# Projections of a fused LayerNorm, attention and LoRA layer: GpSimd in program order, T sums one product ahead, fixed places for the own sums, token operands stored one transfer at a time

## The chip, the cores and the metric

The kernel runs on one core of a Trainium2 chip. The metric is the device time of one launch in microseconds; the median of three runs counts. All arithmetic is in float32.

The engines are named as in the profile: PE multiplies matrices (PEld loads its stationary operand), DVE, ACT and POOL (GpSimd) work on elements, and SP issues most of the transfers (DMAs). Each engine takes its instructions in a fixed order and waits on semaphores.

## The reference

```python
xn = layernorm(x)                       # x: 4 x 512 x 1024
qkv = xn @ w_qkv                        # 32 query heads, 8 key/value heads of 128
scores = einsum(q, k) * 128**-0.5 - slope * sqrt(distance)   # causal
attn = softmax(scores) @ v @ w_o        # grouped heads
ffn = xn @ W.T + b + LoRA(xn)           # rank 8, 16, 32 or 64 by the top gate
out = x + attn + ffn
```

## The kernel before, in words

The kernel has three parts one after the other: `project()` (LayerNorm, the gate and the projections to q, k and v), `attend()` (attention) and `finish()` (W and w_o). The change lies in the first part, and in two loads of the second.

**Two levels of Strassen-Winograd.** Each large product is computed from seven products of half size instead of eight, and each of those again. The outer level works on a pair of batches (1024 tokens): the products are numbered 1 to 7 and taken in the order `PROJECTED`, (1, 2, 6, 3, 7, 4, 5). The inner level makes seven multiplications out of each product: class `Inner`, methods m1 to m7, each of them four 128x128 by 128x256 matrix instructions in the profile. `run()` (L172) calls them in the order m1, m5, m4 of the product before, m6, m3, m2, m7, and calls `beside()` after each. So a product is seven multiplications, and a *set* is seven products, 49 multiplications. There are 24 sets, twelve for each pair of batches: for each two key/value heads one set "kv" (keys in column 0, values in column 1), then two sets "q".

**Sums.** Winograd's scheme needs sums of operands:
- *outer sums of tokens*: `Pair.outer` and `Pair.inner`, on DVE (one on POOL), once for a pair; a1 to a7 and their inner sums stay in SBUF for the twelve sets.
- *outer sums of weights*: `outer_w` (L494), eight DVE operations of 128x512 in a set, in tiles `to` and in place in `w`.
- *T sums*: `inner_w` (L513), four POOL operations of 128x256 for each product, in the tile `ti`, which has three buffers. In the version before, `item()` (L526) calls it when the product begins.
- *read-outs*: an inner product's results are read from PSUM by ACT (`scalar.copy`) where there is no base (products 1 and 5), else added to the base by DVE (L127). Product 5 is also added to u and v by POOL, quarter by quarter (L564).

PSUM has two banks for each of the kinds c, d and a. m6 and m7 and m4 accumulate into the bank that m1, m6 and m7 have left, so they wait until that was read out.

**Work put beside the products.** `beside()` (L603) takes steps from queues of generators, so the place of everything in the program is fixed by counting multiplications:
- `soon`: token sums and the transposes of the first pair, on two of three multiplications.
- `weights`: outer sums of weights, a step on each third multiplication.
- `later`: a step on each sixth (`pace[1]`). In it are the routing of each batch, `put_by` (L439) for each of the seven outer operands of a pair (it stores the operand and its inner sums to DRAM, tiles `s`, for `finish()`), and the eight tiles of the second pair (`tile_of_second`, L667: load, LayerNorm, transposes, low rank, store). When product 1 of set 11 is finished, `flush(later)` (L844) emits all that is left of it at once.
- `apart`: two generators `weights_put_by` (L685), turn 0 with its sums on POOL and turn 1 on DVE. They make the *own sums*: sums of W and w_o that `finish()` will want. There are 55 pieces for each. A piece is a load to a tile `wr`, a pause of five multiplications, four sums of 128x256, and a store to `t` or `m`. POOL's are held back during products 1 and 5 (`pace[4]`), DVE's on each third multiplication. They run in sets 1 to 10 and 13 to 23 (`pace[3]`).
- `delayed`: `in_while(n, f)` calls f n multiplications later: loads of the next set's weights `w` (2 MB), stores of q, k and v.

**Order of the engines.** `project()` keeps PE and SP in program order from the start; DVE is added after set 1 (`in_order`, L771, entered at L848). POOL's order is chosen at compile time by the scheduler of the language, from its own estimates; only the own sums and their transfers, under `pin`, keep their order among themselves.

## Time and profile before

| what | us |
|---|---|
| median of three runs | 2808.44 (2808.34 to 2816.88) |
| the profiled execution's own time | 2813.63 |
| its span | 2811.8 |
| PE busy over the span | 2631.7 (94%) |
| POOL busy | 1912.9 (68%) |
| DVE busy | 1766.8 (63%) |
| end of the projections, start of attention | about 1220 |
| mean granted clock of PE | 0.977 |

In what follows a *row* of a timeline has: start in us, duration in us, engine, line, operation, output and input by the program's names, shapes, count, and in brackets the idle time of the engine ahead of it and what ended it. A row of transfers has: output and input, the queue, count, size of one, and the median time in us from issue to landing. Tile names: `ti` T sums, `to` outer sums of weights, `wr` own sums, `s` stored token operands, `xi` and `x` token operands, pc, pd and pa the PSUM banks.

### The profile page before, as it was taken

The page shows a single profiled execution, that of the slowest core. Times are in us where ns is not written, and L with a number is a line of the kernel's source. Part 1 is how long each engine was busy: PE and PEld are TensorE (multiplying, and loading weights), DVE is VectorE, ACT ScalarE, POOL GpSimd, SP SyncE. Part 2 cuts the span into 40 slices and gives each one's busy share as a digit, 9 for nine tenths or more (in the row PEclk, how much of TensorE's full clock was granted, in tenths as well). Part 3 has the DMA queues.
Part 4 walks back from the last instruction along what each step waited for, and adds up shares of the span by engine and source line. Part 5 has one row for each costly group of instructions (what it writes and reads, how often), then busy time and mean ns, then how long its engine had stood idle before and what let it go on. Part 6 is the DMA issues. An engine that isn't in the chain of part 4 may idle for free.

```text
span 2811.8 us, 35613 instructions
## 1 busy us (share of the span) xinstructions
PE 2631.7 (94%) x11872; PEld 2091.1 (74%) x11872; DVE 1766.8 (63%) x3636; ACT 651.4 (23%) x1727; POOL 1912.9 (68%) x1973
## 2 busy tenths in 40 slices
PE   7779999988899999989999999999599999999998
PEld 6668888877778888856666666666488888888887
DVE  6746666558566765546666666766565666566554
ACT  3001111110000000056666666664000000000000
POOL 3557877766687888647777777685566567666573
PEclk9989999989999999999999999999799999999999
DMA  3297777766776774235666666766978878788883
GB/s 131 99 349 243 249 248 239 242 199 217 257 251 229 242 238 157 90 124 174 198 216 198 213 213 199 232 236 198 324 267 311 286 276 324 227 310 295 303 293 122
DMA packets 385065, 648.06 MB, mean 230 GB/s; under 512 B 22569, under 2 KB 285481, under 8 KB 375666
## 3 DMA queue, kind: packets, MB, share of 16 engines
q1 hardware_dynamic: 382130, 638.70, 66.6%
q10 hardware_dynamic: 2752, 7.08, 0.7%
q8 instruction: 95, 1.56, 0.2%
q14 instruction: 88, 0.72, 0.1%
HBM read 387.74 MB, written 257.96 MB: 230 GB/s over the span
## 4 chain that ended last, share of the span: by engine, by line
PE 50%; POOL 5%; DMA 5%; DVE 3%; issue 2%; SPq 1%; ACT 0%; POOLq 0%; ACTq 0%; DVEq 0%
PE pc L1161 11%; PE psc L925 9%; PE po L963 9%; PE pd L1161 5%; PE ptr L950 3%; PE pa L1161 3%; PE pc_q L534 3%; DMA sa<-s 2%; DMA w<-in_w_o_dram 1%; POOL t L130 1%; PE pc_kv L534 1%; PE pd_q L534 1%; DVE pt L953 1%; DVE p L930 1%; PE pd_kv L534 1%
## 5 line engine op out<-in xcount | busy, mean ns | idle before, releaser
L939 POOL TENSOR_SCALAR p<-p,tot 128x256 f32<-128x256 f32 (+3 forms) x512 | 315.5, 635 | 150.6 <-DVE tot L937 93.1
L925 PE MATMUL psc<-k,q 128*128 128x512 f32 (+3 forms) x1024 | 307.5, 439 | 8.2 <-DMA q<-q 7.1
L930 DVE CUSTOM_DVE_ANT_0 p<-psc,bias 128x256 f32<-128x256 f32 (+3 forms) x512 | 245.3, 491 | 104.1 <-PE psc L925 80.3
L130 POOL TENSOR_TENSOR t<-w 128x640 f32<-128x640 f32 x96 | 191.5, 1995 | 171.5 <-DMA w<-in_w_o_dram 74.8
L934 ACT ACTIVATE p<-p,low 128x256 f32<-128x256 f32 (+3 forms) x512 | 283.8, 555 | 72.1 <-DVE low L930 62.5
L963 PE MATMUL po<-pt,v 128*128 128x512 f32 x640 | 290.6, 592 | 0.0
L925 PEld LDWEIGHTS psc<-k,q 128*128 128x128 f32 x1024 | 173.6, 191 | 108.5 <-issue 64.1
L130 POOL TENSOR_TENSOR t<-w,t 128x640 f32<-128x640 f32 x96 | 203.9, 2124 | 35.8 <-PE pc L1161 32.0
L130 POOL TENSOR_TENSOR wr<-wr 128x256 f32<-128x256 f32 x220 | 174.5, 793 | 69.3 <-DMA wr<-in_w_o_dram 24.2
L534 PE MATMUL pc_q<-x,ti_q 128*128 128x256 f32 x704 | 185.0, 386 | 28.8 <-DVE q L127 14.3
L950 PEld LDWEIGHTS ptr<-ident,p 128*128 128x128 f32 x1280 | 147.3, 141 | 73.2 <-issue 40.0
L963 PEld LDWEIGHTS po<-pt,v 128*128 128x128 f32 x640 | 116.8, 190 | 108.5 <-issue 99.2
L534 PE MATMUL pc_q<-xi,ti_q 128*128 128x256 f32 x640 | 169.1, 387 | 20.3 <-DVE q L127 11.3
L953 DVE COPY pt<-ptr 128x512 f32<-128x512 f32 x192 | 129.7, 683 | 83.6 <-PE ptr L950 83.4
L950 PE MATMUL ptr<-ident,p 128*128 128x128 f32 x1280 | 167.7, 274 | 6.0 <-DVE pt L953 4.6
L534 PEld LDWEIGHTS pc_q<-x,ti_q 128*128 128x128 f32 x704 | 134.5, 193 | 51.6 <-DVE q L127 15.5
L130 DVE TENSOR_TENSOR wr<-wr 128x256 f32<-128x256 f32 x220 | 126.5, 575 | 68.5 <-DMA wr<-t 23.3
L534 PEld LDWEIGHTS pc_q<-xi,ti_q 128*128 128x128 f32 x640 | 121.9, 193 | 43.0 <-POOL ti_q L130 13.4
L130 POOL TENSOR_TENSOR ti_q<-w_q 128x256 f32<-128x256 f32 x128 | 103.2, 823 | 69.1 <-PE pc_kv L534 34.0
L165 ACT COPY m<-pc 128x256 f32<-128x256 f32 x30 | 11.2, 372 | 595.1 <-PE pc L1161 595.1
L1161 PE MATMUL pc<-sa,w 128*128 128x256 f32 x480 | 113.8, 385 | 27.9 <-DMA sa<-s 27.9
L130 POOL TENSOR_TENSOR ti_q<-to_q 128x256 f32<-128x256 f32 x96 | 75.9, 803 | 77.9 <-PE pc_q L534 50.8
(296 smaller groups left out, 5857.4 us busy)
## 6 DMA issues: line engine op xcount, KB each, us to landing
sa<-s SPq DMA_DIRECT2D x96, 640.0 KB, 7.7
s<-ot SPq DMA_DIRECT2D x112, 384.0 KB, 5.0
m<-wr SPq DMA_DIRECT2D x70, 512.0 KB, 3.5
w<-m SPq DMA_DIRECT2D x28, 1280.0 KB, 6.9
w_q<-in_w_qkv_dram SPq DMA_DIRECT2D x16, 2048.0 KB, 10.8
q<-q SPq DMA_DIRECT2D x30, 1024.0 KB, 7.1
s<-os SPq DMA_DIRECT2D x48, 512.0 KB, 4.4
t<-wr SPq DMA_DIRECT2D x40, 512.0 KB, 4.1
```

The source lines that it names most:

```text
L130: return eng.tensor_tensor(dst, u, v, ALU.subtract)
L165: nc.scalar.copy(dst, src)
L534: nc.tensor.matmul(dst, ops_w[m][:, c, :], XI[i][m][:, c, :], start=start and c == 0, stop=c == 1, skip_group_check=True,)
L925: nc.tensor.matmul(sc[:, :n], Q[u][:, g, ts(i, P)], K[u][:, :n], start=True, stop=True)
L930: nc.vector.tensor_tensor_reduce(pr[:, g], sc[:, :n], bias[p, h][:, g, S - n :], -SCALE, BIG, ALU.add, ALU.min, low,)
L934: nc.scalar.activation(pr[:, g], pr[:, g], AF.Exp, bias=low, scale=-1.0, accum_out=tot[:, g : g + 1])
L939: nc.gpsimd.tensor_scalar(pr[:, g], pr[:, g], tot[:, g : g + 1], 1.0, ALU.mult, ALU.mult)
L950: nc.tensor.transpose(tr[:, ts(g, P)], PR[u, i][:, g, ts(j, P)], ident)
L953: nc.vector.tensor_copy(pt, tr)
L963: nc.tensor.matmul(po, V[u][:, j, :], PT[i, j], start=(j == 0), stop=(j == i))
L1161: nc.tensor.matmul(bk, w[:, k], x[:, k], start=start and k == 0, stop=stop and k == KB - 1, skip_group_check=True,)
```

## The change

It does these things, all in `project()` but the last:

1. POOL is added to the engines that keep program order.
2. T sums are written by `ahead()` one multiplication after the product *before* has begun (and for product 1 of a set, in product 5 of the set before); `item()` takes them from `inner`. Sets 0 and 1 begin without this.
3. `OWN` lists the multiplications of a set on which outer sums of weights are made; DVE's own sums are held back on just these. While `pace[0]` is 2 (the first two sets) an outer sum is made on each multiplication.
4. POOL's own sums are held back in product 1 and after the fourth multiplication of product 5, and the pause before a piece's store is three multiplications in place of one.
5. `put_by` gives each of its transfers a step of its own, and `later` takes a step on each fourth multiplication in place of each sixth. `routing` and `tile_of_second` get further empty steps; the store of `um` comes two steps after its tile is written.
6. k and v of two heads are stored by one transfer of [128, 2, 512] in place of two, and attention loads half of such a tile.

```diff
-    k_d = {(i, h): scratch(f"k{i}_{h}", [P, S]) for i in range(B) for h in range(NKV)}
-    v_d = {(i, h): scratch(f"v{i}_{h}", [P, S]) for i in range(B) for h in range(NKV)}
+    k_d = {(i, h): scratch(f"k{i}_{h}", [P, 2, S]) for i in range(B) for h in range(0, NKV, 2)}
+    v_d = {(i, h): scratch(f"v{i}_{h}", [P, 2, S]) for i in range(B) for h in range(0, NKV, 2)}
...
         nc.scalar.copy(umT[:RMAX], tr[:RMAX])
-        nc.sync.dma_start(out=um_d[bi], in_=umT)
...
                         nc.sync.dma_start(out=d[:, slot], in_=src)
+                        yield
                     nc.sync.dma_start(out=d[:, 4:7], in_=self.T[i][:, :3])
...
+            inner = {}
+
+            def ahead(st, i):
+                if i > 2:
+                    need_w(st, i)
+                inner[st, i] = inner_w(st, i)
...
-                ops_w = inner_w(st, i)
+                ops_w = inner.pop((st, i), None) or inner_w(st, i)
...
-                        for j in range(2):
-                            d = (k_d, v_d)[col][bi, h + j]
-                            nc.sync.dma_start(out=d, in_=t[:, j, :])
+                        nc.sync.dma_start(out=(k_d, v_d)[col][bi, h], in_=t)
...
-            pace = [1, 6, 0, False, False]
+            pace = [1, 4, 0, False, 0, 0]
+            OWN = (3, 5, 6, 7, 13, 17, 21, 25)
+
+            def own_sums():
+                return pace[2] - pace[5] in OWN
...
-                if pace[2] % 3 == 0:
+                if pace[0] > 1 or own_sums():
                     do(weights)
...
                 u = yield from route(bi)
                 yield
+                yield
                 umT = r4(f"umT_{bi}")[: RMAX + 1, 0, :]
                 masked(bank, bi, u, umT)
+                yield
+                yield
+                nc.sync.dma_start(out=um_d[bi], in_=umT)
                 yield
...
                 xn = xr
+                yield
                 yield
...
                     transposed(bank, xn, t, half, xt[:, half * HC : (half + 1) * HC, :])
                     yield
+                yield
                 low_rank(bank, t, lambda c: xt[:, c, :])
...
-                        while not pace[4] if turn == 0 else pace[2] % 3 == 0:
+                        while pace[2] > pace[4] if turn == 0 else own_sums():
                             yield
                         pin(sub(eng, w[:, k], w[:, u], w[:, v]))
                         yield
-                    yield
+                    yield from pause(3)
...
-            in_order = tc.manual_schedule(engines={PE, SP, DVE})
+            in_order = tc.manual_schedule(engines={PE, SP, DVE, POOL})
...
+                    pace[5] = pace[2]
                     for i in PROJECTED:
...
-                        pace[4] = i not in (1, 5)
+
+                        pace[4] = pace[2] + {1: 0, 5: 4}.get(i, 9)
+                        nxt = PROJECTED[PROJECTED.index(i) + 1 :][:1]
+                        if nxt:
+                            in_while(1, lambda st=st, j=nxt[0]: ahead(st, j))
+                        elif 0 < k < len(sets) - 1:
+                            in_while(1, lambda st=sets[k + 1]: ahead(st, 1))
                         yield item(st, i, accs[st])
...
-                queue.dma_start(out=K[u], in_=k_d[2 * p + bi, h])
+                queue.dma_start(out=K[u], in_=k_d[2 * p + bi, h - h % 2][:, h % 2])
                 queue.dma_start(out=Q[u], in_=q_d[2 * p + bi, h])
-                queue.dma_start(out=VT[u], in_=v_d[2 * p + bi, h])
+                queue.dma_start(out=VT[u], in_=v_d[2 * p + bi, h - h % 2][:, h % 2])
```

## The prediction

> **What bounds the kernel now.** I read the busy rows by stage first, then PE's waits in the projections, then the order of time around the longest of them, then what the SP queue waits for. The projections end at about 1220 us of a 2811.8 us span; the change touches nothing behind them but two loads of attention. In stages (columns: length, busy time of PE, PEld, DVE, ACT, POOL with counts, granted clock, DMA share, GB/s):
>
> ```profile
> 145.00:210.00 65.00, 45.96 (x191) 39.04 (x190) 27.63 (x60) 2.98 (x8) 32.59 (x45) 0.84 1.04 367
> 240.00:590.00 350.00, 336.69 (x1599) 291.25 (x1598) 231.70 (x511) 42.30 (x91) 279.08 (x355) 0.99 0.75 246
> 710.00:760.00 50.00, 40.66 (x176) 34.80 (x175) 25.67 (x55) 2.98 (x8) 32.35 (x41) 0.90 0.89 304
> ```
>
> See that PE bounds the stage (96% in the long middle), except in two short stretches where PE, DVE and POOL are all idle and only the DMA engines are full. There the row says transfers, not arithmetic. PE's waits, projections only, are few; added up from the order of time, PE idles 107 us before 1220: 15.7 in the start-up, 17.2 where DVE is full (75 to 95 and 640 to 700), and the rest singly. The largest:
>
> ```profile
> 171.22 2.08 PE L534 MATMUL pc_q<-xi,ti_q 128*128 128x256 f32 x4 [8.61 <-DVE q L127]
> 195.62 2.07 PE L534 MATMUL pc_q<-x,ti_q 128*128 128x256 f32 x4 [10.43 <-DVE q L127]
> 746.27 2.05 PE L534 MATMUL pc_q<-x,ti_q 128*128 128x256 f32 x4 [8.56 <-DVE u_q L127]
> ```
>
> PE waits for a read-out on DVE, and DVE, in program order, is itself held ahead of it:
>
> ```profile
> 169.95 0.88 DVE L130 TENSOR_TENSOR wr<-wr 128x256 f32<-128x256 f32 x2 [9.87 <-DMA wr<-in_wt_dram]
> 194.38 0.85 DVE L130 TENSOR_TENSOR wr<-wr 128x256 f32<-128x256 f32 x1 [11.25 <-DMA wr<-in_wt_dram]
> 744.70 0.43 DVE L130 TENSOR_TENSOR wr<-wr 128x256 f32<-128x256 f32 x1 [9.56 <-DMA wr<-t]
> ```
>
> So the chain is: a load of own-sum weights lands late, the own sum on DVE blocks, the read-out behind it is late, PE stops. What fills the queue is seen in the issues between 140 and 205 us:
>
> ```profile
> s<-x SPq DMA_DIRECT2D x25, 256.0 KB, 6.4
> s<-xi SPq DMA_DIRECT2D x7, 768.0 KB, 7.6
> t<-wr SPq DMA_DIRECT2D x6, 512.0 KB, 7.6
> ```
>
> These are the token operands of pair 0 (put_by). Between 240 and 590 us, without them, the 512 KB store lands in 3.8 us, not 7.6.
>
> **Part 1: one transfer at a time.** One put_by is 4 x 256 + 768 KB = 1.84 MB. Before, `later` takes a step every 6 multiplications, and a put_by is one step; a multiplication is 0.864 us in an unbroken stretch (x8 matmuls, two of them, in 1.73 us), about 0.9 with the stage's small losses. 1.84 MB in 5.4 us is 340 GB/s on top of 246 - 20 = 226 (the middle row less the second pair's tiles, which come later), 566 against the 390 GB/s that the full slices move. Seven of them last 38 us: 176 x 38 = 6.7 MB too much, 17 us of transfers. PE's stalls there sum to 8.61 + 10.43 + 3.61 = 22.6 us; pair 1 gives 8.56 + 3.34 = 11.9. Together 34.5 us, and the slow clock after them costs more: PE's busy time times what the clock lacks, by slices of 10 us (0.88, 0.77, 0.91, 0.50, 0.91 from 160 us; 0.96, 0.87; 0.56, 0.93; 0.83) is 11 us. Sum 45.
> After, put_by is five steps, one per 4 multiplications: 1.84 MB in 18 us, 102 GB/s. The own sums also go a little slower (16 or 17 multiplications a piece, counted from the generators, for 14 or 15), -13. 226 - 13 + 102 = 315 GB/s: under 390.
> Here a rule speaks against it: the Trainium skill ("DMA: Bandwidth & Descriptors", Specifications) gives the HBM limit of one core as about 358 GB/s. By that the slack is 43 GB/s, and the 2.1 MB weight load of each set, in one burst, stays in the queue nearly as long as the own loads' 5-multiplication lead; residual stalls of some 2 to 3 us a set over 6.5 sets, 16 us. The row shows 354 GB/s as the mean over 65 us and 380 to 410 in its full slices, so slack is 75 and the residue that of today's middle (about 1 us per set) doubled: 10 us. I take 10. **Gain 35** (bounds 20 and 45).
>
> **Part 2: GpSimd in program order, T sums one product ahead.** PE waits for `ti` in the projections for 9.4 us in all (ten stalls of 0.15 to 1.76). By the list of waits POOL itself idles 143 us for PE to release `ti`, so its fixed order had own sums and token sums standing behind T sums that could not start. After, four T sums (0.8 each, 3.2 us) are written at the first multiplication of the product before; their third buffer was released one product earlier, so they wait for nothing of PE's. A product lasts 6.05 us. The tight spot is product 5, with 8 additions of u and v (0.87 each, 7 us): T of the next set 3.2, additions from 5.2 us on as their quarters are read, T of product 2 from 10.4, its first sum at 11.2 against a need at 12.9. It just fits; own sums are closed from the fifth multiplication of product 5 to the end of product 1 for that. **Gain 7** of the 9.4 (bounds 9 and a loss: see the rival). What is queued behind a waiting POOL own sum is now the next T sums and the additions; those waits were 57.8 us in 25 events (2.3 each) before and a product's lead covers them. The four memsets of umT's last row (0.5 us) are ordered too: nothing.
> The SP queue waits 110.9 us on POOL's own sums before their stores (39 times, longest 15.8). pause(3) for one pause puts the store two multiplications later, 1.7 us; I give that no time of its own, it is in part 1's residue.
>
> **Part 3: fixed multiplications.** Outer sums of weights (8 of 0.92 us a set, some on POOL's port) now fall on multiplications 3, 5, 6, 7, 13, 17, 21, 25 in place of each third. 5, 6 and 7 stand together: DVE has 0.92 + 0.42 in 0.864 us there, 1.4 us of delay by the end; m6 of product 2 waits for m1's read-out two multiplications back, which covers about 1 us. So 0 to 0.4 us for 22 sets, 0 to 9; against it, DVE's third-of-three crowding (0.1 to 2 us a stall, 7 us in the middle stage) eases. From both sides -4 to +9; I take a **loss of 2**.
> A second rule bears here: "SBUF — State Buffer", Who interferes with whom, says that a DVE operation with two SBUF inputs is blocked for the whole of a GpSimd one that reads. The row: DVE's own sum is 401 ns at the least, 607 in the middle, 1002 at most. Were every one of 220 blocked fully by 0.73, DVE would have 220 x 0.52 = 115 us more work, and at 65% busy would still not be the bound; but the read-outs, with one input in PSUM, are 418 ns in every row. I take no cost.
>
> **Part 4: the flush.** When product 1 of set 11 is done, all of `later` is emitted at once, into PE's order. Before, steps at one per 6 leave 13 (86 of 99 taken; the last tile from its statistics on, then routing), and the trace shows exactly these: PE stops at 608.3, resumes the products at 623.9, 15.6 us. After, there are 155 steps at one per 4, which leaves 25: tile 14's transposes and low rank, then tile 15 from its load. PE: 6 us for tile 14 (1.97 + 0.6 + 3.68), while the load goes out behind tile 14's store (at about +3) and lands 4.7 later; then the old 15.1 from the statistics: 22.8. That is 7.2 more, of which 3.2 is tile 14's own work, paid before elsewhere; with a longer slow clock (0.57 there) I take a **loss of 6** (4 to 9).
>
> **Smaller edits.** The store of `um`, two steps later, spares SP some of 47.5 us of waiting for `umT`, mostly in the start-up, where DVE is full: 0. The k and v stores become one of 512 KB: one issue less of 0.4 us, on SP, which is not the bound: 0. Attention reads the same 2 KB rows. At pace 2, outer sums at every multiplication move DVE work within a stretch where DVE is full: 0. Set 1's first T sums are not ahead, so its 3.89 us stall stays.
>
> **Sum.** 35 + 7 - 2 - 6 - 2 (unseen joints) = 32. The profiled execution took 2813.6 (span 2811.8): 2782. The median of three runs is 2808.4, 5.2 less: **2776**.
>
> **Rivals.** (a) As above: chance 0.68, 2758 to 2796. (b) More: program order on POOL also ends SP's 110.9 us of waits, and with them the DVE waits of 2 to 4 us in the middle; all of 34.5 + 11 + 9.4 + 10 less the flush's 6, 59 us: 2749; for it speaks the chain of waits, which runs through POOL own sum, store, load at 933 to 966 us; 0.10. (c) The stalls move: at 358 GB/s each weight burst holds own loads, the DVE still blocks for 3 us three times a set, 25 of part 1's 45 stay; with part 2 giving nothing and the flush and part 3 at their worst 45 - 25 - 9 - 9 = 2: 2806, 0.10. (d) Slower: POOL in order blocks on a late own load with T sums and additions behind it. A wait reaches PE from the point where the load lands over 10.4 us after its place in the program: 5.2 us (six multiplications) to the first own sum and 5.2 of the T sums' lead. If all 25 waits (57.8 us) come through, in sets 2 to 10 and 13 to 22, the sum is 32 - 58 = -26: 2834, 0.12; with 55% of them nothing is left of the gain. Against it: a load lands in 4.0 us in the middle, 9.2 at most; for it, that SP can issue it up to 15.8 us late.
>
> **Numbers.** About 0.3% (8.4 us) is what a measurement tells from no change. Slower: (d) 0.12. Within: most of (c), 0.09. Faster 0.79. The range takes (a), (b), and (c): 2745 to 2808.
>
> **What would show it.** Right: DVE's waits for `wr` loads fall from 65 us to under 25, no PE stall over 5 us outside start-up and flush; the stretch 145 to 210 has a clock over 0.95 and under 350 GB/s; PE's waits for `ti` under 3 us; flush stall over 20 us. Wrong: PE waiting for POOL `ti` or for c and u behind a POOL wait of over 5 us, or DVE's waits for `wr` unchanged at 1.5 times the number.

## The result, and the profile after

The change makes the kernel slower: 2848.49 us (2846.19 to 2853.02, 4 runs) against 2808.39 of before beside it, a ratio of 1.0137 (95% interval 1.0114 to 1.016). The forecast was 2776. The profiled execution took 2849.75, its span is 2848.0 and its mean granted clock 0.969 (before: 0.977).

First the stretches of the projections, with one row added for the rest of them (columns as before the change: length, busy time of PE, PEld, DVE, ACT and POOL, granted clock, DMA share, GB/s). This is the kernel after:

```profile
145.00:210.00 65.00, 60.38 (x269) 51.59 (x268) 35.74 (x78) 5.59 (x15) 47.64 (x62) 0.97 0.82 274
240.00:590.00 350.00, 329.30 (x1534) 281.84 (x1533) 214.68 (x484) 42.49 (x91) 268.79 (x339) 0.98 0.72 242
710.00:760.00 50.00, 46.30 (x208) 38.66 (x208) 33.00 (x68) 2.98 (x8) 34.67 (x41) 1.00 0.57 197
760.00:1220.00 460.00, 429.59 (x1888) 365.38 (x1889) 266.83 (x572) 29.79 (x80) 354.82 (x448) 0.97 0.63 213
```

The last row in the kernel before:

```profile
760.00:1220.00 460.00, 441.78 (x2018) 382.41 (x2016) 281.00 (x590) 33.17 (x86) 361.06 (x466) 1.00 0.58 195
```

The two short stretches did what was forecast: the clock is back at 0.97 and 1.00, the traffic under 350 GB/s, TensorE busy. The two long ones, which were sound, got worse: 7 us less of TensorE in the middle, and 12 us less with a clock of 0.97 for 1.00 at the end.

The token operands no longer crowd. Their issues between 140 and 205 us in the kernel after (queue, number, KB each, median us from issue to landing):

```profile
s<-x SPq DMA_DIRECT2D x9, 256.0 KB, 4.6
s<-xi SPq DMA_DIRECT2D x3, 768.0 KB, 5.7
```

But DVE's waits for its own loads, which were to fall from 65 us to under 25, rose to 85 us (us in total, times, longest). Before:

```profile
DVE wr L130 <- DMA wr<-t: 23.3, 7, 9.6
DVE wr L130 <- DMA wr<-in_wt_dram: 22.4, 4, 11.3
DVE wr L130 <- DMA wr<-in_w_o_dram: 19.3, 11, 4.0
```

After:

```profile
DVE wr L131 <- DMA wr<-in_w_o_dram: 43.6, 14, 6.3
DVE wr L131 <- DMA wr<-t: 30.3, 10, 5.9
DVE wr L131 <- DMA wr<-in_wt_dram: 11.3, 4, 4.3
```

No wait is as long as before (6.3 at most, for 11.3), but there are 28 for 22, and they now come in every set that has own sums. Here is one, in the order of time of all engines of the kernel after. It is the boundary between two sets, where SP also issues the 2 MB of the next weights (start, duration, then who; in brackets the idle time before and its releaser):

```profile
920.40 0.73 POOL L131 TENSOR_TENSOR wr<-wr 128x256 f32<-128x256 f32 x1
...
924.04 0.52 SPq L753 DMA_DIRECT2D m<-wr  x1
...
926.08 0.52 DVE L131 TENSOR_TENSOR wr<-wr 128x256 f32<-128x256 f32 x1
...
927.81 0.88 SPq L720 DMA_DIRECT2D wr<-in_w_o_dram  x2
...
928.80 0.52 SPq L753 DMA_DIRECT2D t<-wr  x1
...
929.37 2.09 SPq L408 DMA_DIRECT2D w_kv<-in_w_qkv_dram  x2
...
933.55 2.20 SPq L720 DMA_DIRECT2D wr<-in_w_o_dram  x2
...
942.15 0.47 DVE L131 TENSOR_TENSOR wr<-wr 128x256 f32<-128x256 f32 x1 [4.37 <-DMA wr<-in_w_o_dram]
...
944.14 2.08 PE L543 MATMUL pc_q<-x,ti_q 128*128 128x256 f32 x4 [3.37 <-DVE c_q L128]
```

Read it downwards. GpSimd's store goes out at 924.04, and GpSimd's next load, which goes into the same buffer `wr0`, can be issued only when that store has landed: 927.81. DVE finished its own sums at 926.60, but SP takes its instructions in order, so DVE's store stands behind that load: 928.80. Then come the weights. DVE's next load, again into the same buffer (`wr1`), waits for DVE's store to land: 933.55. It lands 8.6 us later, beside the 2 MB, at 942.15. DVE had been ready since 937.78. Its read-out of `c_q` stands behind the blocked own sum, and TensorE waits 3.37 us for it.

Of TensorE's stalls over 2 us from 160 us on, those before `pc<-x,ti` (the second product of a set) were 6 with 31.5 us before, nearly all in the two crowded stretches; after, there are 15 with 46.4 us, spread over the sets.

**Where the 36 us of the two spans lie.** I counted, in slices of 5 us up to where attention begins (1220 us before, 1260 after), TensorE's idle time, and the slow clock as its busy time times what the clock lacks of 1:

| stretch | idle before | idle after | slow clock before | after |
|---|---|---|---|---|
| 0 to 145 | 32.1 | 33.1 | 4.0 | 7.8 |
| 145 to 240 | 22.7 | 9.5 | 6.2 | 4.0 |
| 240 to 590 | 13.3 | 20.7 | 2.6 | 7.2 |
| 590 to 710 (flush) | 17.4 | 20.8 | 5.1 | 9.2 |
| 710 to 760 | 9.3 | 3.7 | 2.6 | 0.0 |
| 760 to attention | 18.2 | 38.5 | 1.2 | 12.9 |
| all | 113.1 | 126.2 | 21.7 | 41.0 |

The 145 to 240 and 710 to 760 rows gain 24 us; the other rows lose 56. Together that is 32.5 of the 36.2. Over half of the net loss is slow clock, not idle time.

### The profile page after: what moved, and what is told of

Same layout as the page of the kernel before. It is cut to its first block, busy times and chain, and to the rows that moved or that the text cites. A ratio compares the mean times of both kernels' runs of the same rounds, so it can differ in the third digit from the quotient of the medians.

```text
span 2848.0 us, 35667 instructions
## 1 busy us (share of the span) xinstructions
PE 2660.0 (93%) x11872; PEld 2104.2 (74%) x11872; DVE 1764.2 (62%) x3636; ACT 651.2 (23%) x1727; POOL 1929.9 (68%) x1973
## 5 line engine op out<-in xcount | busy, mean ns | idle before, releaser
L956 DVE CUSTOM_DVE_ANT_0 p<-psc,bias 128x256 f32<-128x256 f32 (+3 forms) x512 | 245.4, 491 | 105.5 <-PE psc L951 80.9
L543 PE MATMUL pc_q<-x,ti_q 128*128 128x256 f32 x704 | 191.2, 396 | 37.8 <-DVE c_q L128 29.4
L131 POOL TENSOR_TENSOR wr<-wr 128x256 f32<-128x256 f32 x220 | 162.9, 740 | 91.0 <-DMA wr<-t 25.8
L131 POOL TENSOR_TENSOR ti_q<-w_q 128x256 f32<-128x256 f32 x128 | 112.5, 879 | 55.7 <-PE pc_q L543 32.8
L166 ACT COPY m<-pc 128x256 f32<-128x256 f32 x30 | 11.2, 373 | 592.5 <-PE pc L1187 592.5
L166 ACT COPY q<-pc_q 128x256 f32<-128x256 f32 x64 | 23.8, 372 | 459.7 <-PE pc_q L543 459.7
## 6 DMA issues: line engine op xcount, KB each, us to landing
w<-m SPq DMA_DIRECT2D x28, 1280.0 KB, 11.3
```

The costliest lines, as they stand in the source:

```text
L131: return eng.tensor_tensor(dst, u, v, ALU.subtract)
L166: nc.scalar.copy(dst, src)
L543: nc.tensor.matmul(dst, ops_w[m][:, c, :], XI[i][m][:, c, :], start=start and c == 0, stop=c == 1, skip_group_check=True,)
L956: nc.vector.tensor_tensor_reduce(pr[:, g], sc[:, :n], bias[p, h][:, g, S - n :], -SCALE, BIG, ALU.add, ALU.min, low,)
```

## The experiments

The question was what makes DVE's own loads late in every set. The theories, by the letters that the expectations use: **A**, DVE's sums at fixed multiplications put its load just behind the weight load in every set. **B**, GpSimd in program order does it. **C**, the outer sums on multiplications 5, 6 and 7 crowd DVE. **D**, GpSimd's new spacing (with `pause(3)` and the new rule for `pace[4]`) puts its store and load beside DVE's. **E**, the transfers one at a time and the early steps of `later` hold the queue up. **F**, which replaced A and D as they fell: SP's order together with the landing of stores makes a chain. Its rivals were **G** (the transfers themselves are too slow) and **H** (GpSimd in program order makes its own sums late wherever they stand). In the summary, "waits" are DVE's for its own loads, and idle and slow are counted up to 1260 us, 115.2 and 23.7 for the kernel before. (In the faster kernels this takes in some attention, which starts at 1166 us in h2_f3l3two; in the slower ones the projections end later.)

| run | made from | us | ratio, 95% interval | waits | idle, slow |
|---|---|---|---|---|---|
| e1_w9 | after | 2876.93 | 1.0228 (1.0205 to 1.0251) | 101.6 | 142.0, 47.5 |
| e2_w21 | after | 2946.62 | 1.0489 (1.0462 to 1.0516) | 163.8 | 206.6, 57.6 |
| e3_put | before | 2813.68 | 1.0007 (1.0 to 1.0014) | 57.6 | 108.2, 31.2 |
| e4_own_p3 | before | 2805.41 | 0.9984 (0.9976 to 0.9992) | 59.3 | 105.5, 30.1 |
| e5_nopool | after | 2838.76 | 1.0099 (1.0073 to 1.0124) | 79.7 | 122.2, 42.7 |
| e6_gp1 | after | 2877.23 | 1.0242 (1.0223 to 1.026) | 104.7 | 137.5, 50.9 |
| e7_chain | before | 2860.44 | 1.0177 (1.0162 to 1.0192) | 101.5 | 136.8, 43.7 |
| e8_v16 | after | 2910.88 | 1.0359 (1.0342 to 1.0376) | 134.1 | 173.1, 53.7 |
| f1_two | after | 2820.05 | 1.005 (1.0034 to 1.0067) | 63.5 | 106.6, 29.5 |
| f2_btwo | before | 2802.23 | 0.998 (0.9972 to 0.9988) | 41.0 | 108.4, 25.0 |
| f3_e4put | before | 2787.78 | 0.993 (0.9909 to 0.9951) | 38.1 | 88.7, 25.7 |
| f5_gpstore | after | 2904.34 | 1.0349 (1.0333 to 1.0366) | 131.0 | 165.4, 55.4 |
| g1_oldgp | after | 2878.52 | 1.0247 (1.0228 to 1.0267) | 104.9 | 141.1, 50.4 |
| g2_f3l3 | before | 2769.91 | 0.9869 (0.9849 to 0.9889) | 43.1 | 80.3, 15.9 |
| g3_f3two | before | 2779.85 | 0.9901 (0.9884 to 0.9919) | 26.0 | 87.0, 26.4 |
| h1_act | after | 2858.84 | 1.018 (1.0165 to 1.0195) | 93.6 | 130.9, 36.6 |
| h2_f3l3two | before | 2760.82 | 0.9838 (0.9822 to 0.9854) | 30.8 | 71.0, 20.4 |
| h3_l3 | after | 2842.86 | 1.0134 (1.0117 to 1.0151) | 92.5 | 123.2, 38.3 |

**The place of the weight load (e1_w9, e2_w21).** The kernel after with `in_while(4, ...)` at 9 or at 21:

```diff
-                        in_while(4, lambda k=k: W.update({sets[k + 1]: load_w(sets[k + 1])}))
+                        in_while(9, lambda k=k: W.update({sets[k + 1]: load_w(sets[k + 1])}))
```

> The changed kernel with one number different: the next set's weights (2 MB) are loaded 9 multiplications after a set begins, not 4. DVE's own-sum load then goes out ahead of them (its place is multiplication 7 of every set). Theory A (the new spacing locks DVE's own sums to the set, so that one of their loads stands behind the weight load in every set): the stalls in product 2 (47 us in 18 sets, and some 20 us of slow clock after them) go; about 2780. Theory B (GpSimd in program order makes its stores, and so SP, late): the weight load's place is nothing; 2848 within 10. Theory C (the outer sums at multiplications 5, 6, 7 crowd DVE): 2848 within 10.

> The changed kernel with the weight load at multiplication 21: now DVE's second load of the set (multiplication 24, first sum at 29) stands behind it as its first did. Theory A: the stall moves to product 5 and stays as large; 2848 within 15, and not under 2830. If only the early place were bad (the outer sums of theory C beside it), it would fall to about 2790. Theory B: 2848 within 10, with the stall still in product 2.

Both are slower, and slower than any of the theories had it. At 9 TensorE no longer stops in the second product but in a later one, mostly for 4 to 8.3 us at a time. At 21 it stops for 3.4 to 11 us. So the weight load's place matters, but nothing is gained by moving it alone: another own transfer is then late. (In e1_w9 one DVE store of each set leaves 3.6 to 9.2 us behind DVE's last sum.) Theory A fell here in its simple form.

**The parts on the kernel before (e3_put, e4_own_p3, e7_chain).** e3_put takes over only the transfers one at a time (with the later steps and one step in 4 that go with them). e4_own_p3 takes over only the fixed multiplications, for the outer sums of weights and DVE's own sums, with the longer pause for DVE. e7_chain is e4_own_p3 with GpSimd's new spacing as well:

```diff
-                    yield from pause(3 if turn else 1)
+                    yield from pause(3)
...
-                        pace[4] = i not in (1, 5)
+                        pace[4] = pace[2] + {1: 0, 5: 4}.get(i, 9)
...
-                        while not pace[4] if turn == 0 else own_sums():
+                        while pace[2] > pace[4] if turn == 0 else own_sums():
```

> The kernel before with only the token operands stored one transfer at a time, `later` at each fourth multiplication and the further empty steps. Theory D: the predicted gain of this part alone, 25 to 35 less 6 for the longer flush; 2775 to 2795. Theory E: 2830 or more.

> The kernel before with only the fixed multiplications for the outer sums and for DVE's own sums, and the longer pause ahead of DVE's stores: these lock DVE's loads to multiplications 7, 24 and 40 of each set. GpSimd's order, the T sums and the token stores are those of before. Theory A: slower by the 47 us of stalls and their slow clock, 2850 to 2870. Theory B: 2808 within 10, since GpSimd is untouched. Theory C: slower too, but with stalls behind outer sums and not behind a DVE own sum that waits for its load.

> The kernel before with the fixed multiplications, the longer pause ahead of both stores and GpSimd's new hold in products 1 and 5: the same spacing of own-sum transfers as in the changed kernel (GpSimd's stores 15, 31, 47, DVE's 3, 20, 36), with GpSimd's order, T sums and token stores of before. Theory D: slower than before, 2835 to 2865. Theory E: no slower than the run with DVE's part alone (2805), within 10.

e4_own_p3 ends theory A: DVE locked to fixed multiplications, its load behind the weights in every set, and not slower than before. C fell with it, as the outer sums stand on 5, 6 and 7 there too, and E with e3_put, which is not slower. (e3_put is not the gain that D had for it either.) e7_chain brings theory D to the front: GpSimd's spacing, and nothing else, makes 2805 into 2860. e3_put gains its stretch (145 to 240: idle 22.7 to 9.8) and gives it back in the long ones (240 to 590: 13.3 to 18.0).

**The parts taken out of the kernel after (e5_nopool, e6_gp1, e8_v16).** e5_nopool has no program order for GpSimd and no T sums ahead (the lines that call `ahead` are gone too); e6_gp1 has `pause(3 if turn else 1)`; e8_v16 starts DVE's own sums eight multiplications later.

```diff
-            in_order = tc.manual_schedule(engines={PE, SP, DVE, POOL})
+            in_order = tc.manual_schedule(engines={PE, SP, DVE})
...
-                    yield from pause(3)
+                    yield from pause(3 if turn else 1)
...
-                yield from pause(8 * turn)
+                yield from pause(16 * turn)
```

> The changed kernel without program order on GpSimd and without T sums ahead. Theory A: 2848 to 2858, as GpSimd's part was worth up to 9 us of gain. Theory B: back to 2815 or less.

> The changed kernel with GpSimd's pause ahead of its stores back at one multiplication (DVE's stays at three). GpSimd's stores then stand at multiplications 13, 27, 41 and its loads at 17, 31, 45, as before; in the changed kernel they stand at 15, 31, 47 and 2, 19, 35, so that DVE's stores (3, 20, 36) follow one multiplication after a GpSimd load. Theory D (each load waits on the SP queue until the store of the same buffer has landed; with the two spaced like this DVE's load comes two landings in a row after GpSimd's store, later than the 14 multiplications to its first sum allow): the stalls behind late own-sum loads go back to those of before; 2785 to 2810. Theory E (one transfer at a time and the early `later` steps hold the queue up): no change, 2848 within 10. Theory B (GpSimd's order): no change.

> The changed kernel with DVE's own sums begun 16 multiplications late, not 8: by count both stores then stand at the same multiplication (15, 31 or 32, 47 or 48) and both loads at 2 or 3, 19, 35 or 36, so one landing serves both. Theory D: most of the stalls go; 2800 to 2825. Theories B and E: 2848 within 10.

Theory D in its simple form (undo the pause, or move DVE aside, and it is well) fell twice: e6_gp1 and e8_v16 are both slower, with a long stall in nearly every set (2.1 to 8.4 us, in a later product, in e6_gp1; 3.9 to 7.7 us in e8_v16). e5_nopool lies between what A and B had for it. GpSimd's order seemed worth only 10 us here; g1_oldgp, below, shows that this holds only where its spacing has done the damage already.

**The landing (f1_two, f2_btwo).** A second buffer for `wr0` and `wr1`, so that a load need not wait for the store before it. The room is taken from `r4`.

```diff
-            counts = {"w": 2, "ti": 3, "r4": 7, "m1": 2, "m5": 2, "m6": 2}
+            counts = {"w": 2, "ti": 3, "r4": 5, "m1": 2, "m5": 2, "m6": 2, "wr0": 2, "wr1": 2}
```

> The kernel after, with two buffers for each engine's own sums instead of one, so that a load of the own sums no longer waits on SP for the store before it to land (the 4 KB a row that this needs twice come from r4, which has 5 buffers for 7). Theory F (SP takes its transfers in program order, and the wait of a load for the landing of the store before it holds up everything behind it, DVE's own load above all): SP's waits of a load for a store's landing, 287 us in the kernel after, fall under 30, DVE's waits for its own loads fall from 85 us under 40, and the time is 2780 to 2810. Rival G (the landing is not what delays the load; the transfers themselves, 2 MB of weights among them, or SP's waits for GpSimd's sums do): DVE's waits stay over 70 us and the time is 2835 to 2855.

> The kernel before with the same two buffers (r4 with 5 for 7). Theory F: SP's 216 us of waits of a load for a store's landing go, DVE's waits for its own loads fall from 65 us under 40, and the time is 2780 to 2800. Rival G: nothing of the time hung on the landing; 2803 to 2815.

The kernel after goes from 2848 to 2820: 28 of the 40 us are back, with one buffer count. SP's waits of a load for a store's landing, 287 us, are gone. The waits fell from 85 to 64 us only, and the time missed 2810, so F is right as to most of it and not all. What eats into the gain: a 512 KB load now takes 5.6 to 5.9 us in the median, for 3.9 to 4.2, and SP waits 254 us for GpSimd's sums, for 170.

The total of the landing waits is not the measure, though: it is 216 us before, 287 after, but 295 in e4_own_p3 and 306 in f3_e4put, the version of 2788 us below. What counts is which of them stand in front of a DVE transfer. The kernel before gains 6 us by the same edit (a little short of the 8 expected at the least).

**Who issues (f5_gpstore, h1_act).** GpSimd issues its own stores, or ScalarE issues DVE's own loads and stores:

```diff
-                    pin(nc.sync.dma_start(out=dst, in_=w))
+                    pin((nc.sync if turn else nc.gpsimd).dma_start(out=dst, in_=w))
...
-                            pin(nc.sync.dma_start(out=w, in_=src))
+                            pin((nc.scalar if turn else nc.sync).dma_start(out=w, in_=src))
```

(The second line stands for all four issues of own transfers in h1_act.)

> The kernel after, but GpSimd itself issues the store of its own sums, behind them in its own order, instead of SP. SP then waits no longer for GpSimd's sums (170 us in the kernel after). Theory F in its narrow form (this wait at the head of SP's queue is what delays DVE's load): DVE's waits fall under 50 us, the time is 2790 to 2815. In its wide form (the landing of stores does it, whoever issues them): DVE's waits 65 to 85 us, the time 2830 to 2850. A third case (a store issued by GpSimd lands later than one of SP's, and GpSimd's next load with it): over 2850.

> The kernel after, with the loads and stores of DVE's own sums issued by ScalarE instead of SP. SP then holds GpSimd's, and DVE's loads stand behind nothing of GpSimd's. Theory F (DVE's store and load are late because they stand on SP behind GpSimd's store and load): DVE's waits for its own loads fall from 85 us under 45 and the stalls of TensorE in the second product go. The time is then 2790 to 2820, if ScalarE's own work isn't held up by the waits that its queue takes over; over 2830 if it is, with TensorE's stalls behind ScalarE's evictions in their place. Rival G (the transfers themselves are slow): DVE's waits over 65 us.

The narrow form of F (the head of SP's queue, and it alone) fell in both. In f5_gpstore SP's waits for GpSimd's own sums are gone (170 us to 4), and its waits of loads for landings rise from 287 to 440: the next load, still on SP, now waits for the sums and the landing together. The time is that of its third case, but not for the reason given there, since GpSimd's stores landed in 3.3 us. In h1_act the waits are 94 us. Its ScalarE (ACTq is what ScalarE issues):

```profile
883.62 0.53 ACTq L753 DMA_DIRECT2D m<-wr  x1
...
892.75 0.37 ACTq L727 DMA_DIRECT2D wr<-t  x1
893.22 0.37 ACT L166 COPY u_q<-pc_q 128x256 f32<-128x256 f32 x1 [8.49 <-DMA m<-wr]
```

and its DVE:

```profile
880.38 0.52 DVE L131 TENSOR_TENSOR wr<-wr 128x256 f32<-128x256 f32 x1
...
897.35 0.42 DVE L131 TENSOR_TENSOR wr<-wr 128x256 f32<-128x256 f32 x1 [5.27 <-DMA wr<-t]
```

DVE's last sum ends at 880.90. The store goes out 2.7 us later behind ScalarE's own work, the load waits 8.49 us for its landing (SP issued 2 MB of weights at 882.53), and the load takes 4.6. GpSimd is in none of it, and the sum is as long as on SP. That fits the Trainium skill ("DMA: Bandwidth & Descriptors", Issuing engines are not separate DMA queues): DMAs of every issuing engine run on the same 16 DMA engines, and another issuer saves only issue time. h1_act swaps one engine's order for another's, though, so it doesn't clear SP: it shows that leaving SP is not enough.

**The two halves together (f3_e4put), and GpSimd's order by itself (g1_oldgp).** f3_e4put is e3_put and e4_own_p3 in one. g1_oldgp is the kernel after with GpSimd's own sums spaced as before; it differs from f3_e4put by GpSimd's program order, the T sums ahead and the joined k and v stores.

```diff
-                    yield from pause(3)
+                    yield from pause(3 if turn else 1)
...
-                        pace[4] = pace[2] + {1: 0, 5: 4}.get(i, 9)
+                        pace[4] = i not in (1, 5)
...
-                        while pace[2] > pace[4] if turn == 0 else own_sums():
+                        while not pace[4] if turn == 0 else own_sums():
```

> The kernel before with the transfers one at a time, and DVE's own sums at fixed multiplications with the longer pause for DVE alone; GpSimd's own sums and its order are those of before. Each half by itself was 2813.7 and 2805.4. Theory F: neither half delays DVE's own loads, so the gain in the stretch 145 to 240 (12 us less idle time of TensorE) stands; 2790 to 2808. Rival G (what the transfers one at a time save comes back later, as in the half by itself): 2805 to 2818.

> The kernel after, with GpSimd's own sums at the places that they had before (the rule of before for their spacing, and one multiplication between the last of them and the store for three); GpSimd's program order and the T sums one product ahead stay. Theory F with the spacing as cause: 2785 to 2805, near the 2788 of the version that has neither. Rival H (GpSimd in program order makes its own sums late wherever they stand, and SP waits for them): SP's waits for GpSimd's sums over 150 us and the time 2815 to 2860.

f3_e4put beats before by 20 us, more than its halves (+2 and -4). With GpSimd in order 2788 becomes 2879, more than even H had for it; the wait that H named is there (239 us, against over 150). D, which had the spacing as the cause of everything, fell. What SP waits for, in f3_e4put:

```profile
SPq L745 <- POOL wr L130: 65.3, 31, 15.5
```

in g1_oldgp:

```profile
SPq L753 <- POOL wr L131: 238.6, 36, 15.9
```

and what GpSimd itself waits for in g1_oldgp:

```profile
POOL v_q L128 <- DVE r_q L128: 90.4, 16, 11.5
...
POOL v_kv L128 <- DVE r_kv L128: 33.9, 7, 5.4
```

In the kernel before, GpSimd waited for DVE's `r` once, 11.5 us. In program order GpSimd stops at an addition whose operand DVE has not read out, DVE stands at an own sum whose load SP has not issued in time, and SP stands at a store whose sums GpSimd has not written: three engines in order, each behind the next. In the order of time, in one set of g1_oldgp:

```profile
943.33 0.84 POOL L128 TENSOR_TENSOR v_q<-v_q,r_q 128x256 f32<-128x256 f32 x1 [5.43 <-DVE r_q L128]
...
957.24 3.78 POOL L131 TENSOR_TENSOR wr<-wr 128x256 f32<-128x256 f32 x4
...
959.83 0.61 DVE L131 TENSOR_TENSOR wr<-wr 128x256 f32<-128x256 f32 x1
...
961.05 0.52 SPq L753 DMA_DIRECT2D t<-wr  x1
...
964.27 1.60 SPq L720 DMA_DIRECT2D wr<-in_w_o_dram  x2
...
966.55 0.52 SPq L753 DMA_DIRECT2D t<-wr  x1
...
972.17 0.37 SPq L730 DMA_DIRECT2D wr<-in_w_o_dram  x1
...
976.01 0.56 DVE L131 TENSOR_TENSOR wr<-wr 128x256 f32<-128x256 f32 x1 [5.49 <-DMA wr<-in_w_o_dram]
...
976.96 2.08 PE L543 MATMUL pd_q<-xi,w_q 128*128 128x256 f32 x4 [4.31 <-DVE q L128]
```

GpSimd reaches its own sums at 957.24, behind the additions and the T sums. SP holds their store until 961.05 and GpSimd's next load until that store has landed, 964.27. Only then comes DVE's store, 966.55, 6.1 us after DVE's last sum; DVE's load follows its landing, 972.17, and DVE and TensorE stop. It is the chain of the kernel after, but later in the set and away from the weights, which had gone out at 945.04. It comes once in each of the 18 sets with own sums: one DVE store leaves 2.8 to 7.4 us late. (In e6_gp1, which has the same order, it is 1.9 to 8.4 us.)

So the spacing and the order can be set against each other (us, and in brackets what SP waits for GpSimd's own sums). All four have the transfers one at a time and DVE's own sums at fixed places; all but f3_e4put have the joined k and v stores:

| GpSimd's own sums | order left to the compiler | program order, T sums ahead |
|---|---|---|
| spaced as before | f3_e4put 2788 (65) | g1_oldgp 2879 (239) |
| spaced as after | e5_nopool 2839 (94) | after 2848 (170) |

Either change alone undoes the gain of f3_e4put.

The boundary between sets in f3_e4put, to hold against the one of after:

```profile
925.79 0.61 DVE L130 TENSOR_TENSOR wr<-wr 128x256 f32<-128x256 f32 x1
926.09 3.65 POOL L130 TENSOR_TENSOR wr<-wr 128x256 f32<-128x256 f32 x4
926.43 0.53 SPq L745 DMA_DIRECT2D m<-wr  x1
927.01 0.62 SPq L401 DMA_DIRECT2D w_q<-in_w_qkv_dram  x1
930.00 0.37 SPq L722 DMA_DIRECT2D wr<-in_w_o_dram  x1
930.47 0.52 SPq L745 DMA_DIRECT2D m<-wr  x1
...
938.82 0.88 DVE L130 TENSOR_TENSOR wr<-wr 128x256 f32<-128x256 f32 x1 [1.84 <-DMA wr<-in_w_o_dram]
...
941.22 1.13 PE L534 MATMUL pc_kv<-x,ti_kv 128*128 128x256 f32 x4 [1.25 <-DVE c_kv L127]
```

DVE's store leaves with the end of its sums (926.40), since GpSimd's store comes only after it (930.47). The load is out at 930.00 and lands 8.8 us later, as late as in the kernel after; but it left 3.6 us after DVE's last sum and not 7.0. From it DVE waits 1.84 us and TensorE 1.25. I took the same from the order of time of the eight sets between 640 and 1200 us (medians, us after DVE's last sum of a set):

| kernel | weights issued | DVE ready for the next sum | it starts | TensorE's time |
|---|---|---|---|---|
| e4_own_p3 | 0.6 | 10.6 | 11.8 | 2805 |
| e7_chain (its GpSimd spaced as in after) | 2.3 | 10.9 | 14.6 | 2860 |
| f3_e4put | 0.6 | 10.6 | 12.1 | 2788 |
| after | 2.5 | 11.2 | 14.7 | 2848 |
| f1_two (after, two buffers) | 0.7 | 11.2 | 12.8 | 2820 |
| e5_nopool (after, GpSimd's order left to the compiler) | 2.1 | 10.9 | 14.6 | 2839 |
| g1_oldgp (after, GpSimd spaced as before) | 0.6 | 11.1 | 11.4 | 2879 |

(The last column is the kernel's time in us.) The store stands right before the weights, so the first column is how late SP gets to it. Where GpSimd's load stands before it and waits for a landing, 2 us are lost there and another 1 to 2 behind it, and DVE's 10.6 to 11.2 us of slack are used up. Two buffers give them back. This is the harm of the spacing. In g1_oldgp this place is clear, and its loss is the chain above.

**Steps left over and the rest of the waits (g2_f3l3, g3_f3two, h2_f3l3two, h3_l3).** `pace[1]` is how many multiplications lie between two steps of `later`: 3 for 4 leaves none at the flush.

```diff
-            pace = [1, 4, 0, False, False, 0]
+            pace = [1, 3, 0, False, False, 0]
```

g3_f3two is f3_e4put with the two buffers, h2_f3l3two has both edits, h3_l3 is the kernel after with a 3 for the 4.

> The version of before with transfers one at a time and DVE's own sums locked (2788), with one spare step in three multiplications less put off, so that fewer steps are left for the flush. If the flush and its stretch 590 to 710 (19 us idle, 8 us slow clock) come from steps left over: 2775 to 2785. If they come from the routing and the loads that stand there anyway: 2783 to 2795.

> The same version (2788) with two buffers for each engine's own sums. Theory F: what is left of DVE's waits for its own loads (38 us) goes; 2775 to 2785. If these waits no longer stop TensorE: 2785 to 2792.

> The version of 2770 (before, with transfers one at a time, DVE's own sums locked, fewer steps put off) with two buffers for each engine's own sums. If the two gains of 18 and 8 us are apart: 2758 to 2766. If the waits for own loads no longer reach TensorE there: 2766 to 2774.

> The kernel after, with one multiplication in three less put off, so that no steps are left over at the flush. If the flush is worth what it was in the version without the own-sum spacing (18 us): 2826 to 2834. If the late own loads hide it: 2840 to 2850. If steps taken more densely put GpSimd's and DVE's sums later still: over 2852.

g2_f3l3 gains 18 us on f3_e4put, more than expected; in 590 to 710 the idle time goes from 19.4 to 9.9 and the slow clock from 8.4 to 0. g3_f3two gains 8, and h2_f3l3two both, apart: 2760.8, the fastest version, 1.6% under before (0.9838). Its long stretches:

```profile
240.00:590.00 350.00, 343.62 (x1673) 300.81 (x1672) 236.03 (x536) 52.43 (x112) 285.09 (x362) 1.00 0.77 251
...
760.00:1220.00 460.00, 449.87 (x2034) 375.41 (x2033) 280.92 (x658) 72.48 (x199) 350.76 (x460) 0.99 0.58 192
```

In h3_l3 the same edit is worth about 6 us (2848.5 to 2842.9; 590 to 710 has 8.7 us less idle time, the late own loads take part of it back). This was between my two readings there.

## Why the prediction was wrong

**Part 1, the crowding: right in its place, smaller in size.** 145 to 240 and 710 to 760 together gained 23.6 us of idle time and slow clock, against 35 (bounds 20 and 45). The clock and the GB/s of the stretches came as written. For the whole kernel the part was worth nothing by itself (e3_put) and 18 us on top of the fixed places of DVE's own sums (e4_own_p3 to f3_e4put). Two readings were off, without weight for the sum: the row of 145 to 210 us has 367 GB/s (354 is the mean of 140 to 205), and DVE's read-outs take 365 to 426 ns, not 418 in every row.

**Two terms failed, and either is enough to lose the gain: the spacing of GpSimd's own sums, put at nothing, and GpSimd's program order, put at a gain of 7.**

**The spacing, put at nothing,** stands at the end of part 2: "pause(3) for one pause puts the store two multiplications later, 1.7 us; I give that no time of its own, it is in part 1's residue." I counted the multiplications of an own sum (16 or 17 for 14 or 15) and never asked at which multiplication of the set each transfer then falls, nor what stands beside it on SP. Counted since from the program, per set of 49 multiplications: before, DVE's transfers drifted through the set with a period of 15, so a bad meeting came now and then. After, all are locked. GpSimd stores at 15, 31 and 47 and loads at 19, 35 and 2; DVE stores at 3, 20 and 36 and loads at 7, 24 and 40; the weights are at 4. Each GpSimd load is one multiplication before a DVE store, so its wait for a landing is in front of DVE's store every time. e7_chain prices this step (the pause and the new rule for `pace[4]`, which were not parted there) at 55 us on e4_own_p3, and e5_nopool at 51 on f3_e4put, both without GpSimd's order; f1_two gives 28 of the 40 back by taking the landing away. The residue that I put at 10 us, from stalls of the weight burst, was these, and more of them.

**Part 2, GpSimd in order, is the second failed term: the gain came, and a price that the sum did not have.** TensorE's waits for `ti` fell from 9.4 to 0.4 us, as forecast. But rival (d) was nearer than the forecast: it said 2834 with "POOL in order blocks on a late own load". The late own load is right, the engine is not: it is DVE that blocks and GpSimd behind it (waits of 105 us for `r` after, 11.5 before), and SP then for GpSimd:

```profile
SPq L734 <- POOL wr L130: 110.9, 39, 15.8
SPq L753 <- POOL wr L131: 169.8, 36, 15.8
```

The first line is before, the second after. GpSimd's waits for its own loads, on which (d) was built, hardly moved (57.8 us before, 65.5 after, 25 times each). Of the reason against (d), "a load lands in 4.0 us in the middle, 9.2 at most", the landing held (3.9 to 4.2 in the median, 8.6 beside the weights). What decided was the point that stood for (d), that SP can issue a load late. g1_oldgp prices the part (with the joined stores) at 91 us against f3_e4put where the spacing is the old one, e5_nopool at 10 where it is the new one.

**Part 3, the fixed multiplications: right in size, the other sign.** I took a loss of 2; by themselves, for DVE alone, they gain 4 to 5 us (e4_own_p3). That locking makes a meeting with a neighbour permanent was missing; it is what e7_chain shows.

**Part 4, the flush: right.** TensorE's stop there went from 15.6 to 25.4 us, for 22.8 forecast. A loss of 6 was forecast; the flush's stretch, 590 to 710, lost 7.5, and taking the left-over steps away gave 6 (h3_l3). That no steps need be left, and that this is worth 18 us where own loads are in time (g2_f3l3), I did not see.

**The signs named in advance.** Four of the five that were to show the forecast right came true: the clock and GB/s of 145 to 210, waits for `ti` under 3 us, a flush stall over 20, and no stall over 5 us elsewhere in the projections (4.97 at most). They watched the gains and the longest stall, and the loss came as many stalls of 2 to 5 us. The fifth did not come. "DVE's waits for `wr` unchanged at 1.5 times the number" was to show the forecast wrong; they were 85 us for 65, with 1.3 times the number (28 for 22). The line was the right one to watch.

**What stays open.** On f3_e4put the spacing alone costs 51 us, GpSimd's order alone 91, both 60: they don't add, and no run says why both together cost less than the order alone. In g1_oldgp, program order, T sums ahead and joined stores were not parted. f1_two is still 32 us over f3_e4put with landings out of the way; its SP waits 254 us for GpSimd's sums, and once in each set with own sums a DVE store leaves 1.7 to 6.3 us behind DVE's last sum, which points to the order, but no run shows what that costs. Why e3_put and e4_own_p3 gain more together than singly is also only guessed: a drifting DVE meets the stretched transfers sooner or later.

## What to carry to other kernels

When a change moves the steps of a queue that works in order, list by place, for one period, every store, load and sum, and ask what each load waits for before it can be issued; a load into the only buffer waits for the landing of the store before it, and everything behind it on the queue waits too. Locking a pattern to fixed places makes its meetings permanent: it pays where the places are clear of each other (e4_own_p3) and costs every period where they are not (e7_chain). Ask too when the engine whose work a store waits for gets to that work: put in program order, it can be late every period as well (g1_oldgp). A second buffer was the cheapest test of that chain, and part of the cure.

## What the runs showed of the hardware

- **A stall can cost more than its length, and there is no sharp point.** TensorE's group of four matmuls takes 1.03 us in an unbroken stretch. Behind the stall of 3.37 us shown above it took 2.08, half the clock, and behind one of 1.25 us in f3_e4put 1.13. But two stalls of the same length in the kernel after went different ways:

```profile
896.12 1.96 PE L543 MATMUL pc_q<-x,ti_q 128*128 128x256 f32 x4 [2.57 <-DVE c_q L128]
...
1088.87 1.13 PE L543 MATMUL pc_q<-x,ti_q 128*128 128x256 f32 x4 [2.57 <-DVE c_q L128]
```

  In the projections of all twenty kernels (160 to 1160 us), a slow group (over 1.5 us for four matmuls) followed none of 135 stalls of 0.9 to 1.8 us (of those with all four matmuls in the trace), 73 of 168 from 1.8 to 4 us, and 105 of 107 over 4 us. The Trainium skill ("TensorE: Matmul & The Clock Gate", Part 1) has the clock fall after an idle window of about 3.4 us; here the shortest stall with a slow group behind it was 1.81 us (e6_gp1). That is how 19 of the 32 us counted above came to be slow clock.
- **A 512 KB own load beside 2 MB of weights** takes 8.6 and 8.8 us (after, f3_e4put) for a median of 3.9 to 4.2 in the kernel after; with the landing of its store out of the way it took 9.9 in one set (f1_two, issued 2.2 us after the weights). DVE was ready for it 4.2 us (after) and 7.0 us (f3_e4put) behind its issue.
- **Letting GpSimd issue its own stores** (f5_gpstore) made these land sooner and SP's remaining ones later: 3.3 us for 512 KB against 5.2 (4.4 for those to `t`), where all landed in 3.8 (4.7 to `t`) in the kernel after. The kernel took 2904 us.
